# A decoder layer on one core: cross-attention weights applied to the context, and feed-forward tokens turned in 32x32 blocks through DRAM

## The chip, the core and the metric

The kernel runs on one core of one Trainium2 chip. A core has five engines with their own queues, each in order: TensorE (PE in the profile, with its weight loads shown as PEld), VectorE (DVE), ScalarE (ACT), GpSimd (POOL) and SyncE (SP), which here issues all DMAs. The metric is the device time of one execution in microseconds; lower is better. Before the change it was 1412.74 us, the median of three runs from 1412.63 to 1412.88.

## The reference, cut to what matters

Eight sequences of 256 tokens, width 1024, everything in f32. `ctx` is the context, 256 rows for each sequence.

```
x = layernorm(x + self_attention(x))                  # 32 heads, 8 key heads, RoPE, causal
Q = x @ Wq.T + bq ;  K = ctx @ Wk.T + bk
x = layernorm(x + softmax(Q @ K.T / 32) @ ctx)        # cross-attention, one head of width 1024
w = lut4[code of 4 bits]                              # 1024 x 1024, made from bit planes
x = layernorm(x + x @ w.T + bias)                     # (a second table where a row is long; no row is here)
```

In cross-attention the scores are h (Wq.T Wk) ctx.T plus terms of the biases. A term that is the same for all keys of a token drops out of the softmax. The kernel therefore multiplies the two weights with each other once, into a 1024 x 1024 matrix M.

## The kernel before, in words

All large products use one step of Winograd's scheme (`winograd`): a product of 2 x 2 blocks by 7 multiplications of half-size blocks instead of 8. For one sequence the seven come in the order 1, 2, 6, 5, 7, 3, 4, and each accumulates in one bank of PSUM, x or z, 128 x 512. After each, VectorE adds the bank into SBUF (`put`, `add`). Products 6, 7 and 4 go on accumulating in the bank x that has just been read, and product 3 in z, so each of them waits for the reading of that bank. Sums of the token blocks that the scheme needs are made by GpSimd (`token_sides`), sums of the weight blocks mostly by VectorE.

A program is written as generators that are stepped beside each other. PE, DVE, ACT and POOL keep program order (`InOrder`), so what a loop emits between two steps is what stands in each queue. DMAs by `nc.sync` are placed in SP's queue by the scheduler. A DMA that waits holds the ones behind it.

1. Stage 1 (to about 340 us): projections of all sequences to queries, keys and values, RoPE on VectorE. Beside it, `dequant_low` makes the feed-forward weights, 128 outputs at a time. It has 40 steps for each 128 outputs: masks and selections on VectorE, eight activations of 128 x 128 on ScalarE for a block of 128 x 128. Finished blocks are turned on VectorE and stored to `wf_d`.
2. Stage 2 (to about 855 us): self-attention, its output projection (`project`), and the product of the cross weights (`weight_product`, stored to `m_d`, loaded back and summed by `cross_weights`). The first `EARLY` = 6 groups of 128 outputs are dequantised here and in stage 1: 195 steps in stage 1 and 45 in stage 2. The weights of the projection lie in seven slots of `w_pool`, w0 to w6.
3. Stage 3 (from 859 us): cross-attention and feed-forward, sequence by sequence. `q_begin` transposes the two tiles of 128 tokens on TensorE: 16 transposes of 128 x 128 into PSUM, four to a bank, and four copies on ScalarE. `q_project` multiplies them with M: 7 products of 16 matmuls with 128 moving columns. `score` multiplies the result with the context, `turn` transposes the probabilities, `values` multiplies them with the context (8 matmuls of 512 columns), adds, normalises and stores the tile to `h2_d`. The remaining two groups of the dequantisation run beside the first `BEHIND` = 4 sequences. From the fifth on, one cross-attention and one feed-forward alternate, and then four feed-forwards follow. `f_begin` transposes the feed-forward's tokens on TensorE as `q_begin` does, makes the sums, squares for the norm and adds the bias on GpSimd. `feed_forward` has 7 products of 4 matmuls with 512 columns.

In the trace each f32 matmul is two instructions, a transpose is one. A product of 16 matmuls is therefore 32 instructions, and one of 4 matmuls of 512 columns is 8.

Of the kernel before, what the change touches and what calls it, by code (L numbers as in the profile page):

```python
# [24 lines left out]
F32 = mybir.dt.float32  # L25
# [17 lines left out]

EARLY = 6
BEHIND = 4
# [21 lines left out]
def decoder_layer(  # L67
# [8 lines left out]
    w_o: bass.AP,  # L76
    wq: bass.AP,
    wk: bass.AP,
    wk_t: bass.AP,
    bq: bass.AP,  # L80
    bk: bass.AP,
# [45 lines left out]
    wkq = const.tile([P, KC], F32, name="wkq")  # L127
# [4 lines left out]
    owns = const.tile([P, NT], F32, name="owns")  # L132
# [10 lines left out]
    h1_d = [dram.tile([P, D], F32, name=f"h1_d{t}") for t in range(NT)]  # L143
    h2_d = [dram.tile([P, D], F32, name=f"h2_d{t}") for t in range(NT)]
# [103 lines left out]
    def weight_rows(w, t):  # L248


        def product(i, ps, start):
            for d in range(4):
                if d == 2:
                    yield
                for k in range(4):
                    matmul(
                        ps[:, ts(d, P)],
                        lhsT=w[i][:, k, ts(d, P)],
                        rhs=t[i][:, k, :],
                        start=start and d == 0 and k == 0,  # L260
                        stop=k == 3,
                        skip_group_check=True,
                    )

        return product
# [19 lines left out]
    def token_sides(side, pool, tag, t, bufs=1):  # L285
# [4 lines left out]
        if side is left_side:  # L290
            return side(pool_e, t[:, 0, low], t[:, 0, high], t[:, 1, low], t[:, 1, high], *sums)
        return side(pool_e, t[:, 0, low], t[:, 1, low], t[:, 0, high], t[:, 1, high], *sums)

    def transpose_rows(dst, srcs):

        for i, half in ((i, half) for i in range(len(srcs)) for half in range(2)):
# [5 lines left out]
            yield  # L302

# [158 lines left out]

    m_stack = ExitStack()
# [3 lines left out]
    def weight_product():  # L467
        def load(n, i):
            if i == 0:
                wk_n = m_pool.tile([P, KC, third], F32, tag="wk", name="wk", bufs=2)  # L470
                sync.dma_start(wk_n, wk[n])
                wks.append(wk_n)
            wq_i = m_pool.tile([P, KC, P], F32, tag="wq", name="wq", bufs=2)
            sync.dma_start(wq_i, wq[i])
            return wq_i

        wks = []
        pieces = [(n, i) for n in range(3) for i in range(KC)]
        loaded = [load(*pieces[0]), load(*pieces[1])]
        for k, (n, i) in enumerate(pieces):  # L480
            yield
            wq_i, wk_n = loaded.pop(0), wks[n]
            ps = bank(m_banks[-1], "xz"[k % 2])[:, :third]
            for q in range(KC):
                matmul(
                    ps,
                    lhsT=wq_i[:, q, :],
                    rhs=wk_n[:, q, :],
# [14 lines left out]
    def bias_dots():  # L503

        bq_bc = m_pool.tile([P, D], F32, name="bq_bc")
        nc.sync.dma_start(bq_bc, bq.partition_broadcast(P))
        rows = [(bk.partition_broadcast(P), bqk)]
        rows += [(wk_t[ts(i, P), :], wkq[:, i : i + 1]) for i in range(KC)]
        for row, to in rows:
# [4 lines left out]
                wide, wide, bq_bc, 1.0, 0.0, op0=ALU.mult, op1=ALU.add, accum_out=to  # L514
# [105 lines left out]
    def begin(b):  # L620
        begun[b] = token_sides(left_side, f_pool, "sx", tokens_of(b), 2)
# [212 lines left out]
    def project(b):  # L834

        a, sums = token_sides(left_side, o_pool, "so", o_ts.pop(b))
# [121 lines left out]
    qs = {}  # L958
    q2s = {}
# [9 lines left out]
    def norm_h(b):  # L969
        for st in range(NST):  # L970
# [3 lines left out]
            uh = c1_pool.tile([P, D], BF16, tag="junk", name="uh")  # L974
            own = owns[:, i : i + 1]
            dve.tensor_tensor_reduce(
                uh, h[b][st], u_bc, 1.0, 0.0, op0=ALU.mult, op1=ALU.add, accum_out=own
            )
            dve.tensor_tensor(own, own, bqk, ALU.add)

    def operands(x):
        return (c_pool, "h_t2", "sf") if x % 2 else (c1_pool, "h_t", "th")

    def q_begin(b):
        pool, whole, sums = operands(min(b, BEHIND))
        h_t = pool.tile([P, NST, KC, P], F32, tag=whole, name="h_t")
        yield from transpose_rows(h_t, h[b])
        qs[b], sums = token_sides(right_side, pool, sums, h_t)
        make(sums)

    def q_project(b):
        q2 = c1_pool.tile([P, KC, S], F32, tag="q2", name="q2")
        q2s[b] = q2

        def put(dh, st, ps):
            to = q2[:, 4 * dh : 4 * dh + 4, ts(st, P)]
            bias = wkq[:, 4 * dh : 4 * dh + 4, None].to_broadcast([P, 4, P])
            dve.tensor_tensor(to, ps.rearrange("p (d s) -> p d s", d=4), bias, ALU.add)

        def add(dh, st, ps):  # L1000
            to = q2[:, 4 * dh : 4 * dh + 4, ts(st, P)]
            dve.tensor_tensor(to, ps.rearrange("p (d s) -> p d s", d=4), to, ALU.add)

        return winograd(p3, weight_rows(mw, qs.pop(b)), put, add, 2)

    def score(b):
        ct_b = c_pool.tile([P, KC, S], F32, tag="ct_b", name="ct_b")
        nc.sync.dma_start(ct_b, c_t[b])
        scale = 1.0 / D**0.5
        q2 = q2s.pop(b)  # L1010
        softs[b] = []

        for st in (1, 0):
            ps = bank(p3, "cross", 3)
            for d in range(KC):
                matmul(
                    ps[:, :S],
                    lhsT=q2[:, d, ts(st, P)],
                    rhs=ct_b[:, d, :],
# [5 lines left out]

            own = owns[:, NST * b + st : NST * b + st + 1]
            nm = small.tile([P, 1], F32, tag="nm2", name="nm2")
            dve.tensor_reduce(nm, ps[:, :S], AX.X, ALU.max, negate=True)
            dve.tensor_scalar(nm, nm, own, own, op0=ALU.subtract, op1=ALU.add)
            dve.tensor_scalar(nm, nm, scale, None, ALU.mult)  # L1030
            pr = c_pool.tile([P, S], F32, tag="pr2", name="pr2", bufs=2)
            sm = small.tile([P, 1], F32, tag="sm2", name="sm2")
            act.activation(pr, ps[:, :S], AF.Exp, bias=nm, scale=scale, accum_out=sm)
# [296 lines left out]
```

## Time and profile before

| what | value |
|---|---|
| median of three runs | 1412.74 us |
| the profiled execution, its own time | 1411.56 us |
| its span in the trace | 1409.8 us |
| granted TensorE clock | 0.99 |
| TensorE busy | 1351.3 us (96%) |
| VectorE busy | 952.3 us (68%) |
| ScalarE busy | 654.4 us (46%) |
| GpSimd busy | 484.2 us (34%) |
| bytes moved by DMA | 153.07 MB, 171322 packets |

The page divides the span into forty slices and lists the costliest groups of instructions. A row of a group gives line, engine, operation, output<-input with shapes and count, then busy time and the mean length in ns, then the idle time before it and what ended it. Nearly all instructions carry the line of the helper (L63), so groups are told apart by names: `tp` is a PSUM bank of transposes, `hf` a tile of the feed-forward, `q` the product with M, `cross` the bank of scores and values, `t`, `m`, `first` and `turned` belong to the dequantisation, `w` to weights. The busy time of a group of matmuls contains their modelled ends, so what a matmul costs in a stream is read from the distance of the starts in the chain of waits. The stage view gives the busy time of each engine in stretches of the span.

### The profile page before, as it was taken

Reading aid. Unit: us, or ns where it says so; the run is one execution under the profiler, and the core shown is the slowest. Engines: PE = TensorE matmul, PEld = TensorE weight load, DVE = VectorE, ACT = ScalarE, POOL = GpSimd, SP = SyncE. Lnnn points to the kernel's source line nnn. Section 1 sums busy time; section 2 is a strip of 40 time slices with the busy share of each in tenths; the row PEclk is TensorE's granted clock in tenths of the full one; section 3 lists DMA queues with packets and bytes.
Section 4 is the critical chain, followed back from the end, with each engine's and each line's share of the span. In section 5 each row is a group of like instructions: output and inputs, shape, how many; then the busy total and the mean of one; then the engine's idle time right before and its main releaser. Section 6 shows DMA issues by size and latency. Waiting matters only on the chain.

```text
span 1409.8 us, 19912 instructions
## 1 busy us (share of the span) xinstructions
PE 1351.3 (96%) x7090; PEld 853.0 (61%) x7090; DVE 952.3 (68%) x1504; ACT 654.4 (46%) x1996; POOL 484.2 (34%) x300
## 2 busy tenths in 40 slices
PE   8999999998999999999999999999899999999996
PEld 4555555555664555555455547898785868674442
DVE  2998888872888878788787865677664343434333
ACT  0455556541877777767767724454312122122120
POOL 1543333310665455354544632011104031223250
PEclk9999999998999999999999999999999999999999
DMA  8345436327731516154133142144281323222201
GB/s 280 67 68 107 81 62 176 56 47 244 283 121 41 185 34 145 45 120 146 19 134 136 46 154 105 38 128 127 93 227 61 135 72 108 88 91 102 78 30 62
DMA packets 171322, 153.07 MB, mean 109 GB/s; under 512 B 131408, under 2 KB 134480, under 8 KB 169296
## 3 DMA queue, kind: packets, MB, share of 16 engines
q1 hardware_dynamic: 171216, 151.73, 37.2%
q8 instruction: 58, 0.95, 0.3%
q14 instruction: 48, 0.39, 0.1%
HBM read 105.54 MB, written 46.15 MB: 108 GB/s over the span
## 4 chain that ended last, share of the span: by engine, by line
PE 77%; DVE 15%; ACT 4%; issue 2%; DMA 1%; SPq 0%; POOL 0%; DVEq 0%; ACTq 0%; POOLq 0%
PE x L63 30%; PE z L63 23%; PE tp L63 9%; PE cross L63 7%; PE u L63 3%; PE v L63 2%; PE sc L63 2%; DVE t L63 2%; ACT pr L63 2%; DVE pr L63 2%; DVE nm L63 2%; DVE st L63 1%; DVE pt L63 1%; ACT t L63 1%; DVE h L63 1%
## 5 line engine op out<-in xcount | busy, mean ns | idle before, releaser
L63 POOL TENSOR_TENSOR pr<-pr,rsum 128x1024 f32<-128x1024 f32 x96 | 187.0, 1949 | 259.1 <-DVE rsum L63 203.0
L63 ACT ACTIVATE t<-first,lt,diff 128x128 f32<-128x128 f32 x512 | 205.7, 482 | 109.5 <-DVE first L63 64.4
L63 ACT ACTIVATE pr<-pr,nm 128x256 f32<-128x256 f32 (+1 forms) x512 | 227.0, 449 | 26.3 <-DVE rsum L63 17.8
L63 DVE TENSOR_TENSOR pr<-sc,causal 128x1024 f32<-128x1024 f32 x96 | 116.7, 1215 | 65.1 <-PE sc L63 21.9
L63 DVE COPY_PREDICATED t<-m,t 128x512 f32<-128x512 int32 (+2 forms) x192 | 147.2, 767 | 2.9
L63 PEld LDWEIGHTS tp<-ident,pr 128*128 128x128 f32 x800 | 93.1, 141 | 78.0 <-issue 42.5
L63 PE MATMUL tp<-ident,pr 128*128 128x128 f32 x800 | 119.0, 278 | 13.0 <-DVE pt L63 7.5
L63 POOL TENSOR_TENSOR ra<-ra,rb 128x512 f32<-128x512 f32 (+1 forms) x48 | 57.8, 1204 | 195.8 <-DVE rb L63 183.8
L63 ACT COPY pt<-tp 128x512 f32<-128x512 f32 (+1 forms) x144 | 77.8, 556 | 97.8 <-PE tp L63 97.7
L63 DVE TENSOR_REDUCE nm<-pr 128x4 f32<-128x1024 f32 (+1 forms) x96 | 117.1, 1220 | 3.3
L63 PE MATMUL x<-wq,xt 128*128 128x512 f32 x200 | 96.3, 605 | 6.6 <-DMA wq<-in_w_q 6.6
L63 ACT COPY h_t<-tp 128x512 f32<-128x512 f32 x64 | 36.9, 585 | 140.9 <-PE tp L63 138.0
L63 POOL TENSOR_TENSOR sf<-h_t 128x512 f32<-128x512 f32 x8 | 10.7, 1343 | 259.0 <-ACT h_t L63 236.6
L63 ACT ACTIVATION_READ_ACCUMULATOR pr<-pr,nm 128x1 f32 x512 | 98.5, 192 | 0.0
L63 ACT ACTIVATE sd<-mv,eps 128x1 f32<-128x1 f32 (+2 forms) x34 | 10.0, 295 | 182.8 <-DVE mv L63 182.8
L63 PE MATMUL x<-w,o_t 128*128 128x512 f32 x192 | 91.7, 602 | 0.8 <-DVE h L63 0.8
L63 PE MATMUL x<-w,h_t 128*128 128x512 f32 x192 | 86.8, 592 | 0.0
L63 PE MATMUL x<-wk,wq 128*128 128x342 f32 x192 | 66.5, 496 | 8.1 <-DMA wq<-in_wq 5.7
L63 POOL TENSOR_TENSOR th<-h_t 128x512 f32<-128x512 f32 x8 | 10.9, 1358 | 156.0 <-ACT h_t L63 156.0
L63 PEld LDWEIGHTS x<-h_t,m 128*128 128x128 f32 x512 | 59.6, 192 | 5.2 <-issue 3.3
L63 PE MATMUL x<-h_t,m 128*128 128x128 f32 x512 | 60.5, 275 | 0.8 <-DVE h L63 0.8
L63 PE MATMUL z<-w,so 128*128 128x512 f32 x128 | 61.1, 602 | 0.0
(157 smaller groups left out, 2566.0 us busy)
## 6 DMA issues: line engine op xcount, KB each, us to landing
h_d<-h SPq DMA_DIRECT2D x32, 512.0 KB, 3.7
wq<-in_wq SPq DMA_DIRECT2D x24, 512.0 KB, 4.8
xt<-in_x_t SPq DMA_DIRECT2D x32, 256.0 KB, 4.4
q_d<-turned SPq DMA_DIRECT2D x128, 64.0 KB, 2.2
q_t<-q_d SPq DMA_DIRECT2D x16, 512.0 KB, 6.1
h<-in_x SPq DMA_DIRECT2D x16, 512.0 KB, 6.2
h<-h_d SPq DMA_DIRECT2D x16, 512.0 KB, 4.4
ct_b<-in_c_t SPq DMA_DIRECT2D x8, 1024.0 KB, 4.9
```

The source lines that it names most:

```text
L63: return lambda *args, **kw: self.tc.keep_in_program_order(issue(*args, **kw))
```

## The change

Three things are done at once.

Cross-attention: M is kept the other way round (weights Wk as the stationary side, Wq as the moving one), and it multiplies the context instead of the tokens. `g_project` takes two sequences at a time, the context of one as the left half of the columns and of the other as the right half, in two parts that each give half of the rows. Each part is 7 products of 8 matmuls with 256 moving columns. The result g goes to DRAM (`g_d`) and is loaded back by `score`. A term per key, the context's rows times a vector, is made by VectorE from rows of the context (`keys`), stored (`key_d`), loaded over all partitions and added to the scores. The term per token is no longer made. The tokens are still transposed on TensorE (`turn_h`), but their sums fall away; GpSimd makes the sums of the context blocks (`g_sums`), 128 x 1024 each.

Feed-forward: at the end of `values` each normalised tile is turned in blocks of 32 x 32 on VectorE (two transposes of 128 x 512), into the space of the context tile `c_b` that was just used, and stored by four DMAs in runs of 32 elements to `ht_d`. `f_begin` loads the transposed tokens by four DMAs in runs of 128 elements in place of the transposes on TensorE and the copies on ScalarE.

Order: `EARLY` is 5, so three groups of outputs are dequantised in stage 3. There are eight rounds u of `g_project`; in round u the attention of sequence i = u - 2 runs beside it, with `values` of sequence i - 1 at step 7 (in the middle of product 5) instead of 8. After the eighth round come the weights' sums, the attention of the last sequences and two feed-forwards, and then six feed-forwards. The slots of `w_pool` hold the context of the pairs, the dequantisation's tiles and then the feed-forward's weights. The last projection of stage 2 has nothing beside it.

```diff
-EARLY = 6
-BEHIND = 4
+EARLY = 5
...
+    def store_turned(key, st, t, space):
+        if key not in ht_d:
+            ht_d[key] = dram.tile([32, NST, KC, 4, P], F32, name="ht_d%d_%d" % key)
+        for half in range(2):
+            dve.transpose(space[:, ts(half, 512)], t[:, ts(half, 512)])
+        for a in range(4):
+            rows = slice(32 * a, 32 * a + 32)
+            nc.sync.dma_start(
+                ht_d[key][:, st, :, :, rows].rearrange("i k c s -> i (k c) s"),
+                space[rows].rearrange("i (kc s) -> i kc s", s=32),
+            )
+
+    def load_turned(key, h_t):
+        for c in range(4):
+            nc.sync.dma_start(
+                h_t[32 * c : 32 * c + 32].rearrange("i t k s -> i (t k) s"),
+                ht_d[key][:, :, :, c].rearrange("i t k s -> i (t k) s"),
+            )
...
+    def g_project(p, part):
+        if part == 0:
+            g_sums(p)
+        pool, tag = ((c1_pool, "g"), (c_pool, "h_t2"))[part]
+        g = pool.tile([P, 2, 2, 2, S], F32, tag=tag, name="g")
...
+        yield from winograd(p3, weight_rows(mw, gs[p], part), put, add, 2)
+        for i in range(2):
+            for dh in range(2):
+                d = 4 * dh + 2 * part
+                nc.sync.dma_start(g_d[2 * p + i][:, d : d + 2], g[:, dh, :, i])
...
     def score(b):
-        ct_b = c_pool.tile([P, KC, S], F32, tag="ct_b", name="ct_b")
-        nc.sync.dma_start(ct_b, c_t[b])
+        g_b = c_pool.tile([P, KC, S], F32, tag="g_b", name="g_b")
+        nc.sync.dma_start(g_b, g_d[b])
...
+            dve.tensor_tensor(pr, ps[:, :S], pr, ALU.add)
-            dve.tensor_reduce(nm, ps[:, :S], AX.X, ALU.max, negate=True)
-            dve.tensor_scalar(nm, nm, own, own, op0=ALU.subtract, op1=ALU.add)
+            dve.tensor_reduce(nm, pr, AX.X, ALU.max, negate=True)
...
             layernorm(tiles[st])
             nc.sync.dma_start(h2_d[NST * b + st], tiles[st])
+        for st in range(NST):
+            store_turned((2, b), st, tiles[st], c_b[:, st])
...
     def f_begin(b):
-        yield from transpose_rows(h_t, hf[b])
-        fs[b], sums = token_sides(left_side, pool, sums, h_t)
+        load_turned((2, b), h_t)
+        yield
+        fs[b], sums = token_sides(pool, sums, h_t)
...
+    for u in range(B):
+        i = u - 2
+        for n, _ in enumerate(g_project(u // 2, u % 2), 1):
...
+            if i >= 0 and n == 3:
+                norm_h(i)
+            if i > 0 and n == 5:
+                turn(i - 1)
+            if i > 0 and n == 7:
+                values(i - 1)
+                fetch_h(i + 1)
+            if i >= 0 and n == 6:
+                begin = turn_h(i)
+            if i >= 0 and n >= 8:
+                next(begin, None)
...
+        if i >= 0:
+            run(begin)
+            run(score(i))
+    b11, b12, b21, b22 = raw
+    t1, t2, t4 = (slot(n) for n in (4, 5, 6))
+    wf, wf_sums = right_side(dve, b11, b12, b21, b22, t1, t2, b12, t4)
+    i = B - 3
+    make(wf_sums, 2)
+    run(turn_h(i + 1))
+    turn(i)
+    values(i)
+    fetch_f(0)
+    fetch_h(i + 2)
+    make(wf_sums)
+    for i in (B - 2, B - 1):
+        j = i - (B - 2)
+        run(in_turn(f_begin(j), score(i)))
+        begin = turn_h(i + 1) if i + 1 < B else f_begin(j + 1)
+        for n, _ in enumerate(feed_forward(j), 1):
+            if n == 2:
+                turn(i)
+            if n == 4:
+                values(i)
+                fetch_f(j + 1)
+            if n == 5 and i + 1 < B:
+                norm_h(i + 1)
+            if n >= 8:
+                next(begin, None)
+        run(begin)
```

## The prediction

> **What bounds the kernel now.** I read the page's engine rows first, then the busy time by stage, then what TensorE waited for, and last the chain of waits through single rounds of stage 3.
>
> ```profile
> PE 1351.3 (96%) x7090; PEld 853.0 (61%) x7090; DVE 952.3 (68%) x1504; ACT 654.4 (46%) x1996; POOL 484.2 (34%) x300
> ...
> 340.00:700.00 360.00, 344.03 (x2276) 198.59 (x2280) 293.51 (x383) 263.35 (x975) 180.18 (x94) 0.99 0.41 120
> 960.00:1000.00 40.00, 34.94 (x261) 32.04 (x260) 26.60 (x55) 19.29 (x45) 5.77 (x4) 1.00 0.36 111
> 1060.00:1200.00 140.00, 140.00 (x753) 101.33 (x753) 57.86 (x116) 29.60 (x58) 35.32 (x25) 1.00 0.27 94
> ```
> The columns of the stage rows are stretch, length, then busy us of PE, PEld, DVE, ACT, POOL, granted clock, DMA share, GB/s. TensorE is the bound, so a microsecond of its work is worth one and other engines count only where TensorE waits for them. From 1060 on it waits for nothing. From 880 to 1060, beside the dequantisation, it lacks 5.8 us of 180.
>
> ```profile
> PE tp L63 <- DVE pt L63: 12.4, 10, 2.3
> PE tp L63 <- ACT pt L63: 6.2, 9, 1.2
> ```
> These are TensorE's largest waits from 340 to 850 us.
>
> ```profile
> 816.48 0.87 PE tp L63 x8
> 859.08 3.84 PE x L63 x32
> 862.91 3.57 PE z L63 x32
> 950.51 3.45 PE cross L63 x8
> 961.67 1.44 DVE t L63
> 963.14 1.24 DVE t L63
> 965.90 0.61 DVE q L63
> 1055.63 0.87 PE cross L63 x4
> 1304.12 3.43 PE x L63 x8
> 1308.00 1.72 PE z L63 x4
> ```
> Chain of waits: start, length, what. A transpose costs 0.87/8 = 0.109 us. A product of 32 instructions with 128 columns takes 3.57 us (0.1116 each), one of 8 with 512 columns 3.43, and an instruction with 256 columns 0.217. Between 1304.12 + 3.43 and 1308.00 lie 0.45 us: four transposes of the next tokens, on the path. At 965.90 TensorE waits for an addition that stands behind the layer norms of `values` and late dequantisation: the kind of wait that decides this case.
>
> **The change part by part.** The sum is against the profiled execution (1411.56 us, span 1409.8); the median is 1.18 above it, and the difference is put on the median. Positions in queues are those of the compiled changed kernel.
>
> 1. Feed-forward transposes leave TensorE: 8 sequences x 16 x 0.109 = -13.9 us, on the path as shown. Their 32 ScalarE copies (0.585) go too. In their place VectorE gets 32 transposes, priced by this row:
> ```profile
> L63 DVE STREAM_TRANSPOSE turned<-ra 128x512 f32<-128x512 f32 x32 | 22.4, 700 | 0.3 <-DMA q_d<-turned 0.3
> ```
> That is 22.4 us of VectorE, 0.175 us for each 128x128 against TensorE's 0.109. The Trainium skill speaks against it: "VectorE: DVE Perf Modes", section "Rules for kernel authors", leaves 128x128 transposes to TensorE, since VectorE only turns 32x32 blocks. By the rule this part loses 8.5 us (22.4 - 13.9), and the sum below would be +15.5 in place of -6.9; by the rows 13.9 are won where VectorE has room, and up to 2.8 lost per sequence where TensorE waits behind it. The trace decides, and item 5 counts those places.
>
> 2. The product with M: 56 products become 16 instructions of 256 columns, 16 x 0.217 = 3.475 for 3.571 us: -0.096 x 56 = -5.4 us. A second reading of the row (6.87 us for 32 instructions of 512, halved) gives 3.435, so the bounds are -5.4 and -7.6. I take -5.4. The 128 transposes of the attention's tokens stay; one sequence's 1.75 us moves from stage 2 to 3.
>
> 3. `EARLY` 5: stage 1 takes 195 steps as before, stage 2 only 5 in place of 45, eight blocks less. Where TensorE waits for `pt` in stage 2, VectorE had mostly just done `t`, `m` or `first`: waits of 2.28, 1.28, 1.28, 1.29, 1.09 and twice 0.34, together 7.9 us. Bounds -8 and 0; I take -6, because some other operation will end part of these waits. The blocks return in stage 3: 24 in seven rounds, 3.4 a round; before, 4 a sequence.
>
> 4. Start of stage 3: two of the context's slots come free after the first two products of the last projection, some 17 us before its end, and the DMA needs 5 to 10 us. The first two products need only loaded blocks (7 us); GpSimd's two sums (1.95 us by its 128x1024 row) fit under them. Cost 0, at most 4 if it starts late. In rounds 0 and 1 VectorE has about 17 us of work under 24.3: 0.
>
> 5. `values` in rounds 3 to 7. Let V be the start of its matmuls. From 950.35 the trace has VectorE's first addition at V+1.9 and both tiles normalised at V+11.3. Now four transposes follow (2.8 us, V+14.1), then what the queue holds (0.72, 0.84, 0, 0.55, 0 us of dequantisation in the five rounds), then the addition of product 5 (0.69). TensorE needs the addition for product 3 at V + 6.87 + 1.73 + 3.46 + 3 x 0.44 = V+13.4. The waits are 2.1, 2.2, 1.4, 2.0 and 1.4: 9.1 us. Before, `values` stood behind that addition. The old 5.8 us fall away: +3.3. Behind VectorE's late addition the later additions are late too, but with 3.5 us of slack each.
>
> 6. The end of round 7, E. The scores of sequence 5 end at E+7.0. The transposes of sequence 6 stand behind exponentials on ScalarE: 2.6 us lost, `values` at E+11.8. VectorE then holds two sums of weights (2.28 each), the layer norms, four transposes, two more sums: free at E+30.6. The scores of sequence 6 (done E+25.6) get their maximum and exponential only at E+34.5, and `turn` on TensorE waits for it behind one product, at E+29.2: 5.3 us. Then in the first feed-forward the addition of product 6 stands behind layer norms, four transposes and two normalisations (0.81 each), V+16.4 against TensorE's V+14.2: 2.2. The context for these `values` can be loaded only when the eight stores of the turned tiles have landed from the same space, about E+33, and comes behind two other 1 MB loads: E+39 to 42 against E+38, 2.5 taken. Sum +12.6. In the second feed-forward +1.5 in the same way.
>
> 7. DMAs. Added per sequence: 8 stores (1024 packets of 128 B), 4 loads, g stored and loaded, context rows, key terms; in all about 8 MB a round of 42 us, where before it was 4. From 200 to 300 us the DMA view has 43942 packets, 42144 of them under 512 B, at half the engines' time; less the large ones at 390 GB/s that is 580 engine-us, or 13.8 ns a small packet. 8192 packets are then 7 us of all engines a round and the rest about 21: 28 of 42. The skill ("DMA: Bandwidth & Descriptors", section "Specifications") wants 512 B for line rate, and the trace agrees: 128 B in 13.8 ns is 148 GB/s. SP issues eight stores at 0.45 to 0.63 us each (`wf_d`, `q_d`), done by V+19, landed by V+22; `c_b` loads by V+33, and the next V is 42 later. `g_b` and the context rows have over 20 us. Cost 0 in the rounds. Loads in 512 B runs are not in the trace; between `xt` (4.2 us for 256 KB) and `w<-wf_d` (8.4), for the second feed-forward, where 7 us of scores cover them, 0 to +3: 0 taken. The others are loaded a whole feed-forward ahead. The key term's addition (0.42) and GpSimd's smaller work lie beside TensorE; ScalarE's copies behind activations +1.
>
> Sum: -13.9 - 5.4 - 6 + 3.3 + 12.6 + 1.5 + 1 = -6.9 us, 1405.8 us on the median.
>
> **The rivals.** A: as above, some 7 us faster. For it: every position is read from the compiled order and every length from a row.
>
> B, slower: VectorE is later than I count, at the seven places where an addition stands behind `values` and the transposes (rounds 3 to 7, the first two feed-forwards). Price: each microsecond there is paid seven times. The point: 1.0 us more a place makes 7 us and ends the gain. For it: at 961.67 two selections took 1.44 and 1.24 us while GpSimd was adding, where the two at 946.62 took 0.79 together; 2 us a place give +14, so 1413 + 7 = 1420. Against it: GpSimd's context sums are over early in a round.
>
> C, better: the transposes find gaps, the end of round 7 loses half of its 12.6, stage 2 gains all 8. About -16: 1397.
>
> D, no change: the DMA queue holds a context tile or a row a few us in each round (5 x 1.4 us), and the gain is gone: 1412.7. For it: SP has some 176 DMAs more in a fixed order (64 stores and 32 loads of turned tokens, 32 and 8 for g, 48 for keys and context), and each wait there holds all behind it. That the products do not get cheaper is no rival: the rows of 256 columns are there.
>
> **How the numbers follow.** Chances: A 0.52, B 0.27, C 0.13, D 0.08. About 0.2% (2.8 us) is what a measurement here can tell from no change. A's own range is 1400 to 1411, so a tenth of it lies within 0.2%. Faster: 0.52 x 0.9 + 0.13 = 0.60 less a little for cases in between, 0.58; same 0.13; slower 0.29. The range 1395 to 1419 leaves out the far half of C and the worst of B.
>
> **What would show it.** In the profile after: `tp<-ident,hf` gone, feed-forward rounds of 24.0 us in place of 25.8; products of 16 instructions in 3.48 us; TensorE's waits for `pt` in stage 2 down from 18.6 us to about 12; in each of rounds 3 to 7 one wait of 1.4 to 2.2 us for VectorE's `g`, and one of about 5 us for ScalarE's `pr` ahead of the second feed-forward product. I am wrong if the waits for `g` are over 3 us each (B), if TensorE waits for DMA in the rounds (D), or if stage 2 is no shorter.

## The result, and the profile after

The changed kernel takes 1416.26 us (median of ten runs, 1412.81 to 1421.29) where the kernel before takes 1412.68 (ten runs, 1410.3 to 1414.27): a ratio of 1.0027, 95% interval 1.0014 to 1.004. It is slightly slower, by 3.6 us; 1405.8 was predicted. The profiled execution of the changed kernel is the fastest of its ten (1412.81 us, span 1411.0), 3.45 us under its median, and that of the kernel before (1411.56) 1.12 under its own. The two profiles therefore differ by only 1.25 us, and the other 2.3 us are spread that only the medians show. The granted clock, averaged over the span, is 0.985 in the profiled execution, 0.9835 in the median of the ten and 0.980 in the slowest; in the profile of the kernel before it is 0.99. As an estimate from these figures, 0.0015 of 1415 us is 2.1 us, so most of what only the medians show goes with the clock.

The engine row of the page, and busy time by stage (columns as in the prediction: stretch, length, busy us of PE, PEld, DVE, ACT, POOL, granted clock, DMA share, GB/s), for the same three stretches as before:

```profile
PE 1339.7 (95%) x6066; PEld 813.7 (58%) x6066; DVE 965.1 (68%) x1535; ACT 637.5 (45%) x1963; POOL 476.6 (34%) x284
...
340.00:700.00 360.00, 355.48 (x2388) 206.28 (x2388) 270.82 (x356) 250.77 (x951) 183.54 (x97) 1.00 0.39 121
960.00:1000.00 40.00, 38.88 (x162) 30.97 (x163) 27.34 (x57) 14.86 (x36) 2.35 (x1) 0.96 0.74 202
1060.00:1200.00 140.00, 124.85 (x485) 87.36 (x483) 88.33 (x159) 34.38 (x73) 12.11 (x6) 0.96 0.83 207
```

In stage 2 TensorE now lacks 4.5 us of 360 where it lacked 16. From 1060 to 1200, where it waited for nothing before, it now lacks 15, the granted clock is 0.96 in place of 1.00, and the DMA engines are busy 0.83 of the time in place of 0.27. Stage 2's last product, before and after, in the chain of waits (start, length, what):

```profile
854.86 3.45 PE x L63 x8
...
836.72 3.45 PE x L61 x8
```

It ends at 840.17 us in place of 858.31: 18.1 us earlier. From there to the end of the span it is 570.8 us in place of 551.5: 19.3 us longer. Most of the gain of one stage was given back in the next.

TensorE's largest waits in stage 2 (340 to 850 us; total, times, longest):

```profile
PE tp L61 <- DVE pt L61: 6.1, 3, 2.7
...
PE tp L61 <- ACT pt L61: 0.2, 1, 0.2
```

and in stage 3 (from 836 us on):

```profile
PE z L61 <- DVE g L61: 9.0, 5, 4.0
PE x L61 <- DVE g L61: 5.0, 2, 3.0
PE tp L61 <- ACT pr L61: 4.4, 2, 3.3
PE cross L61 <- DMA c_b<-in_c: 4.2, 2, 3.7
PE x L61 <- DMA h_t<-ht_d: 2.4, 1, 2.4
PE cross L61 <- DMA g_b<-g_d: 2.3, 1, 2.3
PE x L61 <- DVE hf L61: 1.9, 2, 1.2
```

The first row is the five rounds with `values`: 9.0 us, against 9.1 predicted. The single waits are 4.00, 1.56, 1.30, 1.29 and 0.83, against 2.1, 2.2, 1.4, 2.0 and 1.4, so that the sums agree is luck. The second row, two waits in rounds 0 and 1, was put at nothing in the prediction, and so were those for `h_t` and `g_b`. All waits of TensorE in stage 3 come to 33.5 us; before they were 7.8.

The chain of waits shows a second loss that no list of waits contains:

```profile
851.10 5.38 PE x L61 x16
856.48 3.45 PE z L61 x16
...
892.99 8.86 PE x L61 x32
...
961.12 3.36 PE z L61 x8
...
1139.23 12.84 DMA c_b<-in_c
1152.20 5.38 PE cross L61 x8
...
1276.29 6.87 PE x L61 x16
...
1300.32 6.87 PE x L61 x16
```

A product of 16 instructions takes 3.45 us at 856.48, but 5.38 at 851.10, just behind a wait of 3.0 us. The pair at 892.99 should take 6.91, the half product at 961.12 1.73, the eight instructions at 1152.20 3.45. These four lose 1.93, 1.95, 1.63 and 1.93 us; nine others, mostly behind shorter waits, lose 0.23 to 0.26 each. A fifth slow product does not stand in the chain, which passes to the load of a context tile there. TensorE's queue has it (length as listed, the wait in brackets):

```profile
1177.10 0.69 PE L61 MATMUL tp<-ident,pr 128*128 128x128 f32 x2 [3.25 <-ACT pr L61]
1178.91 0.69 PE L61 MATMUL tp<-ident,pr 128*128 128x128 f32 x2 [1.12 <-ACT pr L61]
1179.39 5.63 PE L61 MATMUL z<-slot,h_t 128*128 128x512 f32 x8
```

In this list such a product has 3.60 where nothing is slow; the granted clock is 0.50 from 1179 to 1182 us, and 2.0 us are lost. Together this is 11.7 us: TensorE mostly runs slowly after it has waited for about 2 us or more. Not always: before, stage 3 was at clock 1.00 up to 1396 us, although TensorE waited 3.81 us ahead of 992.34.

### The profile page after: what moved, and what is told of

The parts are those of the page before. It is cut to its first block, busy times and chain, and to the rows that moved or that the text cites. A ratio compares the mean times of both kernels' runs of the same rounds, so it can differ in the third digit from the quotient of the medians.

```text
span 1411.0 us, 18150 instructions
## 1 busy us (share of the span) xinstructions
PE 1339.7 (95%) x6066; PEld 813.7 (58%) x6066; DVE 965.1 (68%) x1535; ACT 637.5 (45%) x1963; POOL 476.6 (34%) x284
## 4 chain that ended last, share of the span: by engine, by line
PE 77%; DVE 13%; DMA 5%; SPq 2%; issue 2%; ACT 1%; DVEq 0%; ACTq 0%
PE x L61 30%; PE z L61 24%; PE tp L61 10%; PE cross L61 4%; PE sc L61 3%; PE u L61 3%; PE v L61 3%; DVE h L61 2%; DVE st L61 2%; DMA c_b<-in_c 2%; DVE t L61 1%; DVE slot L61 1%; DVE c_b L61 1%; SPq L314 1%; DMA wk<-in_wk 1%
## 5 line engine op out<-in xcount | busy, mean ns | idle before, releaser
L61 ACT ACTIVATE t<-first,lt,diff 128x128 f32<-128x128 f32 x320 | 128.0, 482 | 84.4 <-DVE first L61 51.1
L61 PE MATMUL tp<-ident,pr 128*128 128x128 f32 x800 | 119.2, 278 | 11.1 <-DVE pt L61 6.1
L61 DVE TENSOR_REDUCE nm<-pr 128x4 f32<-128x1024 f32 (+2 forms) x112 | 123.8, 1106 | 3.8
L61 ACT ACTIVATE slot<-slot,lt,diff 128x128 f32<-128x128 f32 x192 | 77.2, 482 | 55.2 <-DVE slot L61 45.5
L61 DVE COPY_PREDICATED t<-m,t 128x512 f32<-128x512 int32 (+2 forms) x120 | 95.0, 792 | 1.9
L61 PE MATMUL x<-slot,h_t 128*128 128x512 f32 x192 | 85.7, 593 | 4.3 <-DMA h_t<-ht_d 2.4
L61 POOL TENSOR_TENSOR slot<-slot,slot 128x1024 f32<-128x1024 f32 x8 | 19.9, 2481 | 175.3 <-DMA slot<-wf_d 67.6
L61 PE MATMUL x<-wq,wk 128*128 128x342 f32 x192 | 65.3, 488 | 7.7 <-DMA wk<-in_wk 5.7
L61 PE MATMUL z<-slot,ms 128*128 128x256 f32 x256 | 61.6, 387 | 9.0 <-DVE g L61 9.0
L61 PEld LDWEIGHTS x<-slot,h_t 128*128 128x128 f32 x192 | 36.2, 190 | 49.3 <-issue 47.2
L61 PE MATMUL cross<-c_b,pt 128*128 128x512 f32 x128 | 58.1, 608 | 4.2 <-DMA c_b<-in_c 4.2
```

Source lines behind the costliest of these rows:

```text
L61: return lambda *args, **kw: self.tc.keep_in_program_order(issue(*args, **kw))
```

## The experiments

Medians are in us. Each set of runs shared its runs of the kernel before (medians 1412.02 to 1413.09); differences between runs are those of their medians, and by the ratios those across sets come out up to 2.1 us smaller or larger, which is said where it matters. "Change" is the kernel with the whole change; the count is n of the loops in rounds and feed-forwards.

| run | median | ratio to before, 95% interval |
|---|---|---|
| before, `EARLY` 5 | 1421.70 | 1.0065 (1.0052 to 1.0078) |
| change, `EARLY` 6 | 1420.32 | 1.0059 (1.0045 to 1.0073) |
| change, TensorE's transposes | 1399.26 | 0.9912 (0.9898 to 0.9926) |
| change, `values` at count 8 | 1419.96 | 1.0054 (1.0041 to 1.0067) |
| change, steps held back | 1410.92 | 0.9986 (0.9976 to 0.9997) |
| change, own space | 1413.84 | 1.0009 (0.9997 to 1.0020) |
| TensorE's transposes + VectorE's unused ones | 1415.39 | 1.0011 (1.0000 to 1.0022) |
| TensorE's transposes + unused stores | 1406.62 | 0.9954 (0.9940 to 0.9968) |
| change, VectorE's transposes at count 8 | 1426.54 | 1.0101 (1.0086 to 1.0116) |
| the same, no key stores | 1405.03 | 0.9946 (0.9933 to 0.9959) |
| change, no key stores | 1410.93 | 0.9984 (0.9977 to 0.9991) |
| TensorE's transposes + unused stores and loads | 1448.53 | 1.0259 (1.0244 to 1.0274) |
| TensorE's transposes, steps held back | 1391.75 | 0.9843 (0.9830 to 0.9856) |
| the same, no key stores | 1391.85 | 0.9851 (0.9838 to 0.9864) |
| TensorE's transposes, steps held back, key rows of 512 B | 1391.19 | 0.9848 (0.9835 to 0.9862) |
| through DRAM, first set of remedies | 1411.15 | 0.9987 (0.9978 to 0.9997) |
| through DRAM, all remedies | 1387.29 | 0.9822 (0.9804 to 0.9841) |

### `EARLY`, alone and undone

In the kernel before:
```
-EARLY = 6
+EARLY = 5
```


> The kernel before with EARLY 5 and nothing else. Theory (EARLY makes the gain of stage 2, and what is lost in stage 3 comes from the other parts): stage 2's last projection ends at about 842 us in place of 858.3, 16 us earlier (18.1 less the 1.75 us of transposes that the full change moves out of it); stage 3 takes the eight blocks, about 20 us of VectorE, beside TensorE and gives back at most 6: 1397 to 1403 us. Rival (the blocks only carry their waits along): stage 3 gives back all 16, 1410 to 1415 us.

Measured: 1421.70. Stage 2 gains 13.6 us (its last product ends at 844.76), and stage 3 loses more than all of it. Both the theory and the rival were too mild. TensorE's waits from 845 us on:

```profile
PE tp L63 <- ACT pt L63: 11.4, 3, 5.7
PE x L63 <- DVE q L63: 7.1, 4, 3.5
```

The dequantisation's eight `t` instructions a block hold ScalarE for 3.2 us at a time, and the copies `pt` stand behind them. 24 blocks in four rounds are six a round, where four had been.

In the changed kernel, the line the other way round:

> The changed kernel with EARLY back at 6. Theory: stage 2 ends at about 856 us in place of 840.2, and stage 3 with 16 blocks in place of 24 loses up to 5 us less to VectorE's lateness: 1426 to 1432 us. Rival (stage 2 is shorter for another reason than EARLY, or stage 3's losses are those of the eight blocks): 1410 to 1418 us.

Measured: 1420.32, between the two theories. Stage 2 ends at 856.14, so `EARLY` 5 is worth 16.0 us there, but the whole kernel is only 4.1 slower: by the medians, stage 3 had paid about 12 of the 16.

### The transposes: on TensorE, on VectorE alone, stores alone

```
-        load_turned((2, b), h_t)
-        yield
+        yield from transpose_rows(h_t, hf[b])
...
-            store_turned((2, b), st, tiles[st], c_b[:, st])
```


> The changed kernel with the feed-forward's tokens transposed on TensorE again: no VectorE transposes, no stores and loads of turned tokens. Theory (the way through VectorE and DRAM costs more than TensorE's transposes): +13.9 us of transposes; the five waits for g in rounds 3 to 7 go (9.0 us and 2.4 of slower products after them), the waits for c_b (4.2 and 2.2) and for h_t (2.4 and 0.2) too: -20.4; together -6, 1406 to 1413 us. Rival (these waits come from VectorE's other work or from the queue and stay): 1424 to 1430 us.

Measured: 1399.26. The theory held and was too small: the way through VectorE and DRAM costs 17.0 us more than the transposes that it saves. TensorE's waits in stage 3 of this run:

```profile
PE x L61 <- DVE g L61: 5.8, 3, 3.0
PE tp L61 <- ACT h_t L61: 3.5, 4, 1.4
PE z L61 <- DVE g L61: 1.7, 1, 1.7
```

The waits for `z` fall from 9.0 to 1.7, and none for DMA is left. Then one part was added back at a time; first VectorE's transposes, into a place that nothing reads:

```
+                dve.transpose(c_b[:, st, ts(half, 512)], tiles[st][:, ts(half, 512)])
```


> As the run with TensorE's transposes (1399.3 us), with VectorE's transposes of the normalised tiles put back into c_b, where nothing reads them: VectorE's share of the turning alone, without its stores and loads. Theory (the additions of g behind the transposes are late): 8 to 12 of the 17 us that the turning cost beside TensorE's 13.9, 1407 to 1411 us. Rival (DMA traffic makes all of it): 1399 to 1402 us.

Measured: 1415.39. VectorE's 21 us of transposes alone cost 16.1 us (14.0 by the ratios), more than expected:

```profile
PE z L61 <- DVE g L61: 9.0, 5, 4.0
...
PE tp L61 <- ACT pr L61: 2.7, 2, 1.4
```

The 9.0 is back to the digit with no turned tile in DRAM. In the two profiles 10.5 us of the difference are longer waits, and most of the rest is slow products; 2.9 us of these stand behind the waits of rounds 0 and 1, which are as long in both runs. From this run to the changed kernel the 13.9 us of TensorE's transposes go, and yet the median rises by 0.9 (2.3 by the ratios). What takes all of it is not separated: the transfers, or TensorE's coming earlier to the same waits. Two runs tried to show the transfers by themselves. In the first the stores read `c_b` as loaded, and the loads went to a spare tile:

```
+            store_only((2, b), st, c_b[:, st])
...
+        load_turned((2, b), spare)
```


> As the run with TensorE's transposes (1399.3 us), with the turned tokens' 64 stores (out of c_b as the context was loaded) and 32 loads (into a tile that nothing reads) put back, without VectorE's transposes: the DMAs' share alone. Theory (the stores hold c_b at the end of round 7 and nothing else): 4 to 8 us, 1403 to 1407 us. Rival 1 (they are hidden): 1398 to 1401 us. Rival 2 (queue and DMA engines hold up more than c_b): 1410 to 1417 us.

Measured: 1448.53, and it settles nothing: the loads, which nothing reads, took places ahead of others in SP's order that they do not have in the change, and TensorE waited 21.2 us for one `g_b`. In the second there are only the stores, out of the normalised tiles:

```
+            store_only((2, b), st, tiles[st])
```


> As the run with TensorE's transposes (1399.3 us), with the 64 stores of 1024 packets of 128 B put back, out of the normalised tiles as they are, with no transposes on VectorE, no loads, and no store out of c_b. Theory (the stores' packets and their time on SP make other transfers late): 4 to 10 us, 1403 to 1409 us. Rival (the stores are hidden where nothing waits for the tile they read; only their hold on c_b costs): 1398 to 1402 us.

Measured: 1406.62. The stores cost 7.4 us (5.9 by the ratios) with no hold on `c_b`, as the theory had it; the one wait for DMA in its profile is 3.5 us for `g_b`.

### GpSimd's sums and VectorE

What makes `g` late in round 0? GpSimd's and VectorE's queues in the changed kernel (start, length, engine, line, operation):

```profile
840.24 4.78 POOL L61 TENSOR_TENSOR slot<-slot,slot 128x1024 f32<-128x1024 f32 x2 [21.44 <-PE x L61]
844.97 2.61 POOL L61 TENSOR_TENSOR slot<-slot 128x1024 f32<-128x1024 f32 x1
847.55 2.39 POOL L61 TENSOR_TENSOR t<-slot,slot 128x1024 f32<-128x1024 f32 x1
...
845.41 2.32 DVE L61 TENSOR_SCALAR slot<-slot 128x256 f32<-128x256 int32 x1
847.66 2.69 DVE L61 TENSOR_TENSOR slot<-qw,bits 128x384 int32<-128x384 int32 x1
850.27 0.68 DVE L61 TENSOR_TENSOR g<-x,wqk 128x512 f32<-128x512 f32 x1
```

Two operations that take 0.29 and 0.55 us elsewhere (at 893.30 and 893.51) take 2.32 and 2.69 here, about one of GpSimd's additions, and they end 0.15 and 0.41 us behind the end of one. The steps were held back:

```
+            held = n < 5 if u == 0 else u % 2 and 8 <= n <= 12
-            while late_done * ...
+            while not held and late_done * ...
```


> The changed kernel; the late dequantisation's steps are held back in the first four counts of round 0 and in counts 8 to 12 of the odd rounds, where GpSimd makes the context's sums, and made up behind them. Theory (VectorE's dequantisation operations stand still while GpSimd adds, and the additions of g behind them are late): the wait of 3.0 us in round 0 and the 1.9 us of slower products after it go, in round 1 waits of 2.0 and about 1 and 1.95 of slower products, in round 3 the wait of 4.0 falls to 2 and the slower products from 1.6 to 0.3: 1402 to 1408 us. Rival (the additions are late for VectorE's other work there): 1413 to 1418 us.

Measured: 1410.92, 5.3 us less, between theory and rival. In round 0 the theory holds completely:

```profile
845.83 0.69 DVE L61 TENSOR_TENSOR g<-x,wqk 128x512 f32<-128x512 f32 x1 [0.42 <-PE x L61]
...
851.10 0.29 DVE L61 TENSOR_SCALAR slot<-slot 128x256 f32<-128x256 int32 x1
```

The addition comes 4.4 us earlier, though stage 2 ended 1.1 later, and the operation behind it takes its 0.29. In round 1 a new wait took the old one's place: VectorE waited 1.5 us for a row of the context (`row`), the steps that had been held back came behind it, and the additions behind those; TensorE waited 2.7 us. In round 3 the steps of count 7 were not held, and the wait of 4.0 stayed. (In the changed kernel a selection takes 2.77 us there, beside a GpSimd addition, where three together take 1.55 elsewhere.)

### The context tile, the stores and the key terms

The turned tiles of sequences 5 to 7 in another space:
```
+        own = c_b
+        if b >= 5:
+            own = c1_pool.tile([P, NST, D], F32, tag="g", name="own")
```


> The changed kernel with a space of its own (that of g's even rounds, free by then) for the turned tiles of sequences 5, 6 and 7, in place of the context's tile c_b. Theory (at the end of round 7 the next context tile is late because it waits for the stores of turned tokens out of the same space): the waits for c_b of 4.2 us and 2.2 us of slower products after them go, 1408 to 1412 us. Rival (the stores and loads ahead of it in SP's queue, or the busy DMA engines, make it late): 1414 to 1418 us.

Measured: 1413.84, 2.4 us less, with intervals that overlap. Its profile still has one wait of 5.1 us for `c_b`, so the hold of the stores on the space is a part at most.

`values` one count later:
```
-            if i > 0 and n == 7:
+            if i > 0 and n == 8:
```


> The changed kernel with values of rounds 3 to 7 after the fourth product (n == 8) in place of in its middle (n == 7). Theory: the addition of product 5 then stands ahead of the layer norms and transposes, and only product 7's stands behind them, due 0 to 0.5 us before VectorE gets to it: the five waits for g go (9.0 us, and 2.4 us of slower products after them), 1403 to 1407 us. Rival (the wait only moves to the next addition, or other work ends it): 1412 to 1417 us.

Measured: 1419.96. The five waits for `z` are gone, as the theory had it, but the time is above theory and rival: TensorE waits 16.6 us for `c_b` instead. Chain:

```profile
1057.40 10.92 DMA c_b<-in_c
1068.45 9.09 PE cross L61 x16
```

The load of `c_b` is issued at 1057.40 and lands 10.9 us later, when TensorE has come sooner. To leave `values` alone, only the transposes and their stores were moved:
```
+            if i > 0 and n == 8:
+                turn_out(i - 1)        # the stores' half of values
```


> The changed kernel with values where it was (n == 7) and only VectorE's transposes and their stores moved behind the next addition: at count 8 in the rounds, at count 6 in the first two feed-forwards. Theory (four transposes of 2.5 us ahead of one addition make the five waits for g): 9.0 us of waits and 2.4 of slower products go: 1402 to 1407 us. Rival (SP's fixed order: with V earlier the context tile is late, as where values stood at count 8): 1412 to 1420 us.

Measured: 1426.54; the rival's cause, and above its range. The waits for `z` fall to 1.7, those for `c_b` rise to 16.1. Chain, and the DMA view of 972.5 to 977.5 us, when SP had issued that load:

```profile
971.39 16.45 DMA c_b<-in_c
...
DMA packets 32, 0.05 MB, mean 10 GB/s; under 512 B 5, under 2 KB 24, under 8 KB 32
...
q1 hardware_dynamic: 32, 0.05, 73.4%
```

The engines are busy for 73% of the time and finish 32 packets. Just ahead of this load SP had issued a store of key terms (SP's queue: start, length, what):

```profile
969.87 0.41 SPq L1067 DMA_DIRECT2D key_d<-per_key  x1
...
971.39 0.45 SPq L1114 DMA_DIRECT2D c_b<-in_c  x1
```

In the changed kernel the same two stand the other way round, in this round (3) and in all others up to 7:

```profile
968.36 0.58 SPq L1114 DMA_DIRECT2D c_b<-in_c  x1
...
970.06 0.48 SPq L1067 DMA_DIRECT2D key_d<-per_key  x1
```

Such a store is 1 KB in 256 packets of 4 B and takes 11.1 us to land in this run and 12.1 in the changed kernel (medians). Where `values` or the transposes moved to count 8, the compiled order put it ahead of the context tile in rounds 3 to 7. So the eight stores were replaced by rows of 1 KB of zeros, written long before; the scores then lack the key terms:
```
-        nc.sync.dma_start(key_d[b].rearrange("(t p) -> p t", p=P), both)
+        nc.sync.dma_start(key_d[b].rearrange("(o s) -> o s", o=1), causal[P - 1 :, :])
```


> The changed kernel with the eight stores of key terms (256 packets of 4 B each, from one column a tile) replaced by rows of zeros in one packet of 1 KB, long before stage 3: the scores lack the key terms. Theory (the stores of 4 B packets hold the DMA engines, 13 to 14 us to landing, and with them c_b, h_t and g_b): the waits for DMA, 8.9 us and 4.5 of slower products after them, fall by half, 1408 to 1413 us. Rival (they only wait in the queue like the rest): 1414 to 1418 us.

Measured: 1410.93, 5.3 us less. The waits for DMA fall only from 8.9 to 6.9 us and not by half, and the two profiles differ by 1.8 us; the rest of the 5.3 shows in the medians alone.

> The run with VectorE's transposes behind the next addition (1426.5 us), with the key terms' stores replaced as in the run beside it. Theory (as there; in the 10 us in which c_b was late in round 4 the engines were busy at 2 to 48 GB/s): the waits for c_b fall from 16.1 to under 8 us, 1408 to 1416 us. Rival (c_b waits for the 1024 packets of each turned tile and for its place behind them in SP's order): 1422 to 1428 us.

Measured: 1405.03, 21.5 us less. The waits of this run:

```profile
PE x L61 <- DMA h_t<-ht_d: 6.3, 1, 6.3
...
PE cross L61 <- DMA c_b<-in_c: 4.1, 1, 4.1
```

8 KB of key terms in 4-byte packets had cost 21.5 us where they stood ahead of the context tile, and 5.3 in the change itself. Without them the same move of the transposes wins 5.9 us (1410.93 to 1405.03), where with them it lost 10.3. That the packets hold the engines is a reading of the DMA view; shown is that the waits for `c_b`, 16.1 us, fall to 4.1 with the stores away. In a kernel without turned tiles they cost nothing:

> The fastest so far (TensorE's transposes, held steps, later rows; 1391.75 us) with the key terms' stores replaced in the same way. Theory: no transfer is late there, so nothing is won: 1390 to 1393 us. Rival (the stores delay g or rows there as well): 1384 to 1389 us.

Measured: 1391.85 for 1391.75.

### What a wait of TensorE costs behind itself

```
+        for _ in range(k):
+            dve.tensor_tensor(scr[:, :512], scr[:, :512], scr[:, 512:], ALU.add)
+        matmul(ps[:1, :1], lhsT=scr[:, :1], rhs=ones, start=True, stop=True)
```


> The changed kernel with ten waits put into the last feed-forwards (sequences 2 to 6, behind the second product and in the middle of the sixth): TensorE waits for a chain of one to eight additions of 128x512 on VectorE (0.6 to 0.69 us each), 1 to 6 us long. Theory (a wait of TensorE of about 3 us or more is followed by some 3.8 us at half clock): the products behind waits of 3 us and more take 1.6 to 2 us longer, those behind waits of 1 to 2.2 us about 0.25 us; the ten waits are 32 us and 8 to 12 us of slower products: 1455 to 1465 us. Rival (the slow products of stage 3 come from the engines and transfers beside them): no product is slower, 1448 to 1452 us.

Measured: 1472.88 in one run, above theory and rival; the waits came to 41.1 us and not 32, as VectorE's additions of 0.69 us took up to 1.8 each while GpSimd was adding. Two of the ten (wait in brackets, then the product of 3.43 us behind it), and the granted clock behind the second (eighth figure from the left of the stage row, ahead of DMA share and GB/s):

```profile
1260.19 0.19 PE L61 MATMUL tp<-ones,scr 128*1 128x1 f32 x2 [1.53 <-DVE scr L61]
1260.31 3.70 PE L61 MATMUL x<-slot,th 128*128 128x512 f32 x8
...
1292.64 0.19 PE L61 MATMUL tp<-ones,scr 128*1 128x1 f32 x2 [3.93 <-DVE scr L61]
1292.76 5.36 PE L61 MATMUL x<-slot,sf 128*128 128x512 f32 x8
...
1292.80:1296.00 3.20, 3.20 (x6) 1.47 (x5) 0.00 (x0) 0.00 (x0) 3.20 (x3) 0.50 0.40 106
```

| wait, us | 1.53 | 1.78 | 2.51 | 3.23 | 3.93 | 4.21 | 4.69 | 5.60 | 6.14 | 7.43 |
|---|---|---|---|---|---|---|---|---|---|---|
| more in the products behind | 0.20 | 1.89 | 1.89 | 1.68 | 1.86 | 1.87 | 3.17 | 2.38 | 2.19 | 2.90 |

The sum is 20.0. From the product at 1245.15 us in the changed kernel (1241.13 here) to the end, this run is 64.1 us longer; the waits, these 20.0 and 3.1 for the small matmuls themselves make 64.2. The clock was 0.50 behind the wait shown. That products are slow behind a wait held, and the rival did not; the threshold of 3 us did not hold, as 1.78 us were enough here. In the changed kernel, of the waits ahead of products, those of 1.98, 2.99, 3.69 and 4.00 us cost 1.6 to 2.0 behind them, and so did that of 3.25 with two transposes between, but two of 2.26 and 2.41 only 0.23 and 0.24. The length alone does not decide: the same wait of round 1, 1.97 to 1.98 us, is followed by a lower clock (0.57 over 4 us) in the changed kernel and four more profiles (VectorE's unused transposes; its transposes at count 8, with and without key stores; change without key stores), and by full clock (1.00) in six (TensorE's transposes; `values` at count 8; own space; unused stores; unused stores and loads; this run).

### Put together

```
+            held = n < 5 if u == 0 else u % 2 and 7 <= n <= 12
...
-            if n in (1, 6, 12):
+            if n in (1, 8, 14):
                 next(of_keys, None)
```


> As the run with TensorE's transposes (1399.3 us), with the late dequantisation's steps held back in the first four counts of round 0 and in counts 7 to 12 of the odd rounds (7 in place of 8, because one block's steps stood behind values), and the key terms' rows read at counts 1, 8 and 14 in place of 1, 6 and 12, so that an addition of g does not stand behind a row that is still on its way. Theory: round 0's 3.0 and 1.9 us, round 1's wait, and the waits of 1.7 us in round 3 and about 1.3 in round 5 go: 1389 to 1394 us. Rival (the steps made up at the end of the rounds make ScalarE or VectorE late there): 1396 to 1403 us.

Measured: 1391.75. Only 2.9 us of waits for `g` are left. The same was then done for the way through DRAM, which had trouble of its own; to the edits above comes:

```
+            if n == 1 and u == B - 2:
+                fetch_wf(0, 2)
```


> The transposes behind the next addition as in the run beside it, with the dequantisation steps held back and the key rows read later as there, the turned tiles of sequences 5 to 7 in a space of their own, and the loads of two of the feed-forward's weight blocks issued at the start of round 6. Theory (with VectorE out of the way the turning through DRAM keeps most of its 13.9 us): 1387 to 1394 us. Rival (the queue of DMAs holds a context tile or turned tokens): 1398 to 1412 us.

Measured: 1411.15; the rival. One context tile was 11.8 us late, and key reductions in their new place, 2.7 us long beside GpSimd, stood ahead of additions (waits for `g` of 8.8 us, where the kernel with TensorE's transposes has 2.9). Then both ways were built with key terms in packets of 512 B and reductions where nothing waits:
```
+        transpose(tp[:NST, :P], both, ident)
+        act.copy(causal[:NST, :P], tp[:NST, :P])
+        nc.sync.dma_start(key_d[b].rearrange("(t p) -> t p", p=P), causal[:NST, :P])
...
+            if n == 13:
+                next(of_keys, None)      # then the next sequence's first row is loaded
```


> The turning through DRAM with all that was found: transposes on VectorE behind the next addition, own space for sequences 5 to 7, dequantisation steps held back, two weight blocks loaded earlier, and the key terms transposed on TensorE (two columns a sequence, in the next round) and stored as two packets of 512 B. Key rows are loaded half a round ahead and reduced at counts 5 and 13. Theory (VectorE's place and the 4-byte stores were the two hosts of the loss): 1387 to 1393 us. Rival (the turned tokens' own stores and loads still hold h_t, g_b and c_b at the end of round 7): 1395 to 1403 us.

> The fastest so far (1391.75 us, TensorE's transposes) with the same key terms: two columns transposed on TensorE, two packets of 512 B, rows loaded half a round ahead and reduced at counts 5 and 13. Theory: no transfer was late there; the reductions no longer stand before an addition, so of the 2.9 us of waits for g one or two go: 1389 to 1392 us. Rival (the key terms' wait on TensorE, or the reduction ahead of values, costs as much): 1392 to 1395 us.

Measured: 1387.29 (1384.75 to 1391.26) and 1391.19 (1390.99 to 1392.21). The first is the fastest of all. Its largest waits in stage 3:

```profile
PE cross L61 <- DVE rs L61: 3.5, 1, 3.5
PE x L61 <- DMA h_t<-ht_d: 2.9, 1, 2.9
```

None is for `z` or `c_b`. The turning through DRAM is worth 3.9 us there, of the 13.9 it takes off TensorE; in the changed kernel it cost 17.0. The size of the 3.9 is uncertain, as the two intervals touch, and the faster kernel also has the own space and the earlier weight blocks. Which of the remedies did how much was not separated.

## Why the prediction was wrong, point by point

The parts made cheaper were read rightly. What failed was the price of the turning through VectorE and DRAM. The sum has it as no loss, 13.9 us won against 13.8 of waits; measured, it cost 17.0 net. The terms that were missing or put at nothing are the transfers (item 7), GpSimd's sums beside VectorE (item 4), and the slow products behind each longer wait (no item).

- **Item 1.** The transposes left TensorE: a feed-forward round takes 24.03 us (1276.29 to 1300.32), 24.0 was predicted. Wrong was to book 13.9 as gain and to leave its costs scattered over items 5 to 7. The terms 9.1, 2.2 and 2.5 there make the 13.8. VectorE's transposes alone cost 16.1 (14.0 by the ratios), and the stores alone 7.4 (5.9). The rule that the item set aside gave the right sign for this kernel; its 8.5 us, reckoned from engine time, are half the loss. The faster kernel that the sum promised was the rest of the change, and it exists: 1399.26.
- **Item 2.** 3.45 us a product for 3.475: right.
- **Item 3.** Stage 2 was 18.1 us shorter, not 7.75; the waits for `pt` fell from 18.6 to 6.3, where 12 was expected. The bound of 8 failed: it counted only waits whose last VectorE operation was a dequantisation, 7.9 us, and 12.3 us of waits for `pt` went. The other half, that the blocks cost nothing in stage 3, failed as well: about 12 of 16 came back.
- **Item 4.** Named as 0, at most 4. Four sums of GpSimd, 2.4 to 2.6 us each, run from 840.24 to 849.94, beyond the end of the first two products at 848.1; two of 1.95 were counted, and that length was the mean of another 128x1024 row. They stop VectorE's dequantisation, and the same happens in round 1. Waits of 5.0, and 3.9 of slow products; holding the steps won 5.3 back.
- **Item 5.** 9.0 us for 9.1, in the five rounds named, but by luck: round 3 waits 1.9 us longer than counted, with a selection of 2.77 us beside GpSimd ahead of the addition, and the other four 0.1 to 0.7 us shorter. Not counted: 2.7 us of slow products behind.
- **Item 6.** 14.1 us predicted with the second feed-forward. The waits there (`pr` 4.4, `c_b` 4.2, `h_t` 2.4 and 1.6, `g_b` 2.3, `hf` 1.9, `h` 0.7) are 17.5, and 5.1 of slow products come on top.
- **Item 7.** DMAs 0 was wrong. Engine time was put at 28 of 42 us, 0.67, which is the least of what was measured (0.66 to 0.98 between 930 and 1115 us), and it was counted in bytes and 128-byte packets. The 4-byte stores were listed as "key terms" without a price; they cost 5.3.
- **No term at all** stood for the clock: 11.7 us (3.9 + 2.7 + 5.1). The one long wait in stage 3 before (3.81 us) shows no such loss, so the profile before could not have told it.

The account of the profiles: stage 2 gave 10.3 us more than predicted; stage 3 lost 18.5 more, of which 11.7 are slow products and 7.3 further waits (33.5 - 7.8 = 25.7 for 18.4 predicted). That is 0.5 too much; the kernel before has two such products too, of 0.24 each. -6.9 + 8.2 = +1.3, as measured. Of the 2.3 us by which the changed kernel's median lies further above its profile than that of before, the granted clock makes about 2.1 by the estimate above; why it differs between executions stays open. Stage 2 alone ends between 836.6 and 842.4 us in the profiles of kernels that share the change's order up to there, so part of the spread lies ahead of stage 3.

Of the rivals, B named the sign (selections slowed while GpSimd was adding) and D the context tile held in the queue. Both came true in part. Of B's places only round 3's addition was later than A said; rounds 0 and 1, which it did not name, were late for its reason. D's tile was late at the end of round 7, and in the rounds only in the runs that moved VectorE's work.

## What to carry to other kernels

Price a step that is moved off the bounding engine by what then stands behind it on its new engine, and allow for slow time after each longer wait of TensorE: here mostly 1.6 to 2 us for waits of 2 to 4 us, and at times nothing. When one wait is taken away, look for what was only just in time behind it: moving four transposes by one place cost 10 us, because a store of key terms then came ahead of the context tile. A transfer is priced by its packets and by what is queued behind it: 8 KB in 4-byte packets cost 5.3 us and, ahead of context tiles, 21.5; the 8 MB of turned stores alone cost 7.4.

## What the runs showed of the hardware

- TensorE after a wait: behind all nine inserted waits of 1.78 to 7.43 us the products lost 1.7 to 3.2 us at a granted clock of 0.50 to 0.72 in the stretch behind, behind 1.53 us 0.2. A wait of 1.97 to 1.98 us was followed by about half the clock in five profiles and by the full clock in six, and one of 3.81 us in the kernel before by the full clock. The Trainium skill ("TensorE: Matmul & The Clock Gate", section "What's actually happening") has the array fall to half clock after at least one idle window of about 3.4 us that runs free of the kernel. The halving agrees. That at least a whole window must be idle does not: waits of 1.78 and 1.98 us were enough at times. By the page, the changed kernel's waits of 1.98 and 2.99 us would have cost nothing behind them; they cost 3.9.
- VectorE beside GpSimd: 0.29 and 0.55 us became 2.32 and 2.69. The skill ("SBUF — State Buffer", section "Who interferes with whom") says that the two share a port pair, which for some of VectorE's instructions one of them holds for a whole instruction while the other stands still. The lengths agree with that: each operation ends just behind one addition on GpSimd (2.61 and 2.39).
- SP needed 6.5 to 7.7 us to issue the eight stores of a sequence's turned tokens, 0.8 to 1.0 each, where the rows of `wf_d` and `q_d` had suggested 0.45 to 0.63.
